# Layer 3 of a four-layer image network: a 3x3 convolution with 12 products in place of 18, and its weights mixed earlier

## The chip, the cores and the metric

The kernel runs on one core of one Trainium2 chip, in float32 throughout. The metric is the device time of one execution in microseconds (us), the median of several runs. The engines are named as in the profile: PE (TensorE, matrix products; PEld is its loading of weights), DVE (VectorE), ACT (ScalarE), POOL (GpSimd) and SP (SyncE, which here issues DMA transfers). Products are accumulated in PSUM banks and moved to SBUF by DVE or ACT, which is called an eviction. A transfer is issued by the queue of an engine; the SP and ACT queues are hardware queues (q1 and q10 of the profile), the POOL queue is a software queue (q0).

## The reference

Eight images of 512 channels and 32x32 positions go through four layers.

- Layer 0: group norm, q, k, v (512x512 each), attention with 8 heads, three steps `hf = hf + 0.1 * tanh(hf @ inl_w.T + inl_b)`, a projection, and the input added.
- Layer 1: attention over the 1024 positions with 64-wide queries and keys, and the input added.
- Layer 2: upsampling by 2 with a 12-tap filter, a leaky ReLU, downsampling by 2.
- Layer 3, a bottleneck block whose weights are different for each image. This is the layer that changes:

```python
pooled = x.mean(axis=(2, 3))
rw = jax.nn.sigmoid(pooled @ router_w.T + router_b)     # 8 numbers per image
W = jnp.einsum('be,eoihw->boihw', rw, experts)          # inside _cond_conv: 8 experts mixed
out = relu(bn1(conv 1x1, 512 -> 128, with W of w1))
out = relu(bn2(conv 3x3, 128 -> 128, with W of w2))
out = bn3(conv 1x1, 128 -> 512, with W of w3)
return relu(out + x)
```

Per image the mixed weights have 512 + 9 x 128 + 512 = 2176 columns on 128 partitions; one expert set is 128 x 2176, all eight are 8.9 MB.

## The kernel before, in words

**Order of the work.** `tile_sequence` handles the images one after the other through layers 0, 1 and 2 (the loop at L1112). Each image's result z is written to device memory in layer 2; image 7's stays in SBUF. Then layer 3 runs for all eight images (L1253 to L1297). A scheduler orders the instructions of each engine by the program's order and by the buffers that are free; only some stretches are fixed by hand. Each engine takes its own instructions strictly in order. The whole program exists a second time (`shifted=True`), which is run only if a range check fails (`out_of_bounds`, L1218); it does not run on these inputs.

**The large products.** q, k, v, the inner steps, the projection and v of layer 1 go through `product` (L404). It computes a 1024x512x512 product from seven block products, in the order P1, C11, U2, U3, C22, C21, C12, in three pairs of PSUM banks: A for P1 and C11, X for U2, U3 and C21, Y for C22 and C12. After each block product `made` evicts two banks. For q and k (`channels`, L453) P1 and C11 go through ACT and the rest through DVE; U2 and U3 are DVE additions of P1's copy (L467). For v (`positions`, L478) all of it goes through DVE; P1 needs two additions of a bias row for each half (L503, L504). An eviction that comes late holds up the next block product in the same bank. Each of q, k, v takes 24 us of PE.

**Weights of `product`** are summed once, for image 0, and stored in device memory over the POOL queue; POOL does parts of the summing itself (L364, L367). Later images load them over the SP queue (`weight`, L340).

**Layer 2's operators** (`layer2_constants`, L133) are matrices that hold the filter taps. They are built from counters (POOL `iota`), the taps, and some 60 small DVE operations (L158 to about L200), called at L847, at the end of image 0's layer-1 scores. `xT` (L857) follows on PE: each bank is emptied by a DVE addition (L858).

**Layer 3.** `route(0, 7)` (L1167) makes the eight mixing numbers of images 0 to 6: a mean, a matmul with the router's weights (L1174), a spreading to all partitions (L1185), a bias (L1189), a sigmoid on ACT (L1193). The scheduler puts it into image 7's layer 1. All experts are loaded once into SBUF by SP (`load_experts`, L1134; the pieces w1, w2_0, w2_1, w2_2 and w3), during image 7's layers 1 and 2, into buffers as these come free. `mixed(b)` (L1204) mixes the weights for one image: per piece one scaling on ACT (L1211) and seven multiply-adds on DVE (L1213), 5 + 35 instructions. It is called one image ahead, and the scheduler begins image 0's during image 7's layer 2, between its DVE evictions (L1003). Per image, PE then does:

- c1: two halves of 4 products each (`project`, L324), relu on ACT into the inside of a zero-rimmed image, of which there are two;
- c2: for each half of the rows 9 products of 128x128 with 128x512, one for each filter tap (L1272), relu on ACT;
- c3: four blocks of two products (L1286); DVE adds the scaled result to z (L1293), ACT applies the relu (L1296), SP writes the output (L1297).

Each f32 matmul appears twice in the records of the profile: 288 records at L1272 are 144 products, 18 for each of 8 images. The buffers that matter: `big`, 7 of 16 KB a partition; `tmp`, 6 of 2 KB or 4 KB; PSUM pools `ps_sc` (two pairs of banks), `ps_tp` and `ps_mm` (two banks each).

Of the kernel before, what the change touches and what calls it, by code (L numbers as in the profile page):

```python
# [9 lines left out]
F32 = mybir.dt.float32  # L10
BF16 = mybir.dt.bfloat16
AF = mybir.ActivationFunctionType
ALU = mybir.AluOpType
# [24 lines left out]
QR = C // 2  # L38
PARTS = ("A11", "A12", "-A22", "S1", "S2", "S3", "S4")
# [14 lines left out]
def tile_sequence(ctx: ExitStack, tc: tile.TileContext, a: dict, out: bass.AP, shifted: bool):  # L54
# [78 lines left out]
    def layer2_constants():  # L133
# [9 lines left out]
        def iota(name, pattern, base, per_partition=0):  # L143
            t = scratch(name, pattern[0][1])
            nc.gpsimd.iota(
                t, pattern, base=base, channel_multiplier=per_partition,
                allow_small_or_imprecise_dtypes=True,
            )
            return t
# [15 lines left out]
        taps_up = scratch("taps_up", NTAP)  # L165
        nc.gpsimd.dma_start(taps_up, a["up_filter"].partition_broadcast(P))
        nc.vector.tensor_scalar_mul(taps_up, taps_up, 2.0)
        taps_dn = scratch("taps_dn", NTAP)
        nc.gpsimd.dma_start(taps_dn, a["down_filter"].partition_broadcast(P))

        part = iota("part", [[1, 1]], 0, 1)
        tap = iota("tap", [[1, NTAP]], 0)

        def rows_of(name, width):

            row = scratch(f"row_{name}", 1)
            first = iota(f"first_{name}", [[width, (P - 1) // width]], width)
            nc.vector.tensor_scalar(first, first, part, None, ALU.is_le)
            nc.vector.tensor_reduce(row, first, AX.X, ALU.add)
            col = scratch(f"col_{name}", 1)  # L180
            nc.vector.scalar_tensor_tensor(col, row, float(-width), part, ALU.mult, ALU.add)
            return row, col

        def tap_index(name, n, step, base, mul, by):

            t = iota(f"ix_{name}", [[step, n]], base)
            add = scratch(f"add_{name}", 1)
            nc.vector.tensor_scalar_mul(add, by, float(mul))
            nc.vector.tensor_scalar_add(t, t, add)
            return t  # L190

        def outer(op, rows, cols):
# [16 lines left out]
        ur = placed("ur", tap_index("ur", UR, -1, 17, -2, in_r), taps_up)  # L209
        outer(up_op, ur, placed("uc", tap_index("uc", UC, 1, 11, -2, in_c), taps_up))  # L210
        outer(
            up_left_op, ur, placed("ucl", tap_index("ucl", UC, 1, 11 - 2 * EDGE, -2, in_c), taps_up)
# [4 lines left out]
            placed("dr", tap_index("dr", OR, 2, -6, 1, up_rr), taps_dn),  # L217
            placed("dc", tap_index("dc", OC, 2, 0, -1, up_cc), taps_dn),
# [4 lines left out]
            placed("ur63", tap_index("ur63", 1, 0, 10, -2, in_r), taps_up),  # L223
            placed("uc63", tap_index("uc63", 2 * W, 1, 5, -2, in_c), taps_up),
# [3 lines left out]
            placed("dr63", iota("dr63", [[2, 3]], 1), taps_dn),  # L228
            placed("dc63", tap_index("dc63", W, 2, 6, -1, part), taps_dn),
# [19 lines left out]
    pooled = const.tile([P, CC, B], F32, name="pooled")  # L249
    spilled = [spill.tile([C, S], F32, name=f"spill_{run}_{b}", tag=f"spill_{b}") for b in range(B)]  # L250
# [338 lines left out]
    def layer0(b, x, norm, w):  # L589
# [12 lines left out]
        if b == 0:  # L602
            nc.vector.tensor_add(row_bias, row_bias, bias2)
        w["inl"] = weight("inl", b)
        all_of(product(f"k_{b}", w["k"], h, t, channels(f"k_{b}", k, qkv_b[:, CC : 2 * CC])))
        w["proj"] = weight("proj", b)
        early = small.tile([P, 1], F32, tag="early", bufs=1, name=f"early_{b}")
        tc.keep_in_program_order(nc.scalar.activation(early, eps, AF.Exp))
        all_of(product(f"v_{b}", w["v"], h, t, positions(f"v_{b}", v, v_row), rows=True))
        w["v1"] = weight("v1", b)  # L610
        hf = big_tile(f"hf_{b}", [P, CC, S])
# [157 lines left out]
    def layer1(b, x, w, midway):  # L769
# [77 lines left out]
        if b == 0:  # L847
            layer2_constants()
# [249 lines left out]
    with tc.tile_pool(name=f"weights_{run}", bufs=1) as wpool:  # L1098
        w = {}
        held = {"q": weight_quarters("q", tmp("raw_q", S))}  # L1100
# [8 lines left out]
        late_loads()  # L1109

# [20 lines left out]
    WCOLS = 2 * C + 9 * P  # L1131
    experts = {}

    def load_experts(key, n, pool=None):  # L1134
        if pool is None:
            t = big_tile(f"{key}e", [P, NE, n])
        else:
            t = pool.tile([P, NE, n], F32, name=f"{key}e", bufs=1)
        nc.sync.dma_start(t, a[key])
        experts[key] = t  # L1140
# [6 lines left out]

    load_experts("w1", C, pool3)

# [11 lines left out]
    router_w = pool3.tile([P, CC, NE], F32, name="router_w", bufs=1)  # L1161
    nc.gpsimd.dma_start(router_w, a["router_wT"].rearrange("(cc p) e -> p cc e", p=P))
    router_b = pool3.tile([P, NE], F32, name="router_b", bufs=1)
    nc.gpsimd.dma_start(router_b, a["router_b"].partition_broadcast(P))
    rw = const.tile([P, B, NE], F32, name="rw")

    def route(b0, b1):  # L1167

        n = b1 - b0
        mean = pool3.tile([P, CC, n], F32, name=f"mean_{b0}", bufs=1)  # L1170
        nc.vector.tensor_scalar_mul(mean, pooled[:, :, b0:b1], 1.0 / S)
        ps = bank(ps_tp, f"router_{b0}")
        for cc in range(CC):
            nc.tensor.matmul(  # L1174
                ps[0:n, 0:NE], mean[:, cc, :], router_w[:, cc, :],
                start=(cc == 0), stop=(cc == CC - 1),
            )

        apart = pool3.tile([n, n, NE], F32, name=f"apart_{b0}", bufs=1)
        nc.vector.tensor_tensor(  # L1180
            apart, ident[0:n, 0:n].unsqueeze(2).to_broadcast([n, n, NE]),
            ps[0:n, 0:NE].unsqueeze(1).to_broadcast([n, n, NE]), ALU.mult,
        )
        ps = bank(ps_tp, f"routed_{b0}")
        nc.tensor.matmul(  # L1185
            ps[:, 0 : n * NE], ones[0:n, :], apart.rearrange("k b e -> k (b e)"),
            start=True, stop=True,
        )
        nc.vector.tensor_tensor(  # L1189
            rw[:, b0:b1, :], ps[:, 0 : n * NE].rearrange("p (b e) -> p b e", e=NE),  # L1190
            router_b.unsqueeze(1).to_broadcast([P, n, NE]), ALU.add,
        )
        nc.scalar.activation(rw[:, b0:b1, :], rw[:, b0:b1, :], AF.Sigmoid)  # L1193

    route(0, B - 1)


    rims = []
    for i in range(2):
        t = pool3.tile([P, H + 2, W + 2], F32, tag=f"rim_{i}", bufs=1, name=f"rim_{i}")  # L1200
        nc.gpsimd.memset(t, 0.0)
        rims.append(t)

    def mixed(b):  # L1204
        wt = pool3.tile([P, WCOLS], F32, tag="mixed", name=f"mixed_{b}")
        parts = [("w1", 0, C)]
        parts += [(f"w2_{ky}", C + ky * 3 * P, 3 * P) for ky in range(3)]
        parts += [("w3", C + 9 * P, C)]
        for key, at, n in parts:
            src, dst = experts[key], wt[:, at : at + n]  # L1210
            nc.scalar.activation(dst, src[:, 0, :], AF.Copy, scale=rw[:, b, 0:1])  # L1211
            for e in range(1, NE):
                nc.vector.scalar_tensor_tensor(  # L1213
                    dst, src[:, e, :], rw[:, b, e : e + 1], dst, ALU.mult, ALU.add
                )
        return wt
# [19 lines left out]
    z3 = {}  # L1236

    def freed(t):
        if t == 4:
            load_experts("w2_0", 3 * P)  # L1240
            z3[0] = load_z(0)
        elif t == 6:
            for ky in (1, 2):
                load_experts(f"w2_{ky}", 3 * P)
        elif t == 7:
            load_experts("w3", C)

    z_last = layer2(B - 1, halo, freed)
    z_next = z3[0]
    redo = None if shifted else out_of_bounds()  # L1250
    wt_next = mixed(0)
    route(B - 1, B)
    for b in range(B):  # L1253
        z, wt = z_next, wt_next
        if b + 1 < B:
            z_next = load_z(b + 1) if b + 2 < B else z_last
            wt_next = mixed(b + 1)
        h1 = rims[b % 2]
        for g in range(2):
            ps = bank(name=f"c1_{b}_{g}")  # L1260
            project(ps, wt[:, 0:C].rearrange("p (cc o) -> p cc o", o=P), 0, z, g)
            nc.scalar.activation(
                h1[:, 1 + 16 * g : 17 + 16 * g, 1 : W + 1],
                ps.rearrange("p (h w) -> p h w", w=W),
                AF.Relu, bias=bn[0][1], scale=bn[0][0],
            )
        h2 = tmp(f"h2_{b}", S)
        banks = [bank(name=f"c2_{b}_{g}") for g in range(2)]
        for ky, g in ((0, 0), (1, 0), (0, 1), (1, 1), (2, 0), (2, 1)):
            for kx in range(3):  # L1270
                at = C + (3 * ky + kx) * P
                nc.tensor.matmul(  # L1272
                    banks[g].rearrange("p (h w) -> p h w", w=W), wt[:, at : at + P],
                    h1[:, ky + 16 * g : ky + 16 * g + 16, kx : kx + W],
                    start=(ky == 0 and kx == 0), stop=(ky == 2 and kx == 2),
                    skip_group_check=True,
                )
        for g in range(2):
# [87 lines left out]
```

## Time and profile before

| | |
|---|---|
| three runs | 3779.12, 3780.01, 3781.69 us; median 3780.01 |
| the profiled execution | 3779.3 us |
| its span, first to last instruction | 3777.5 us, so 1.8 us lie outside |
| mean granted PE clock | 0.997 |
| busy: PE, DVE, ACT, POOL | 3733.1, 2550.6, 1200.6, 85.2 us |
| image 1's q, k, v start | 462.2, 486.2, 510.2 us |
| layer 3: first c1, last c3 ends | 3529.6, 3767.2 us |

How to read the lines: a line such as "L1272 PE MATMUL c<-rim,mixed 128*128 128x512 f32 x288 | 125.5, 593 | 0.0" gives the code line, the engine, the operation, the output and the inputs by the program's names, the tile shapes, the count of instructions, their busy time in us and the mean duration of one in ns, and the idle time of the engine just before them. In the timeline and in the chain of waits the first two figures are the start and the duration in us; "[6.97 <-DVE up L1003]" says that the engine had stood idle 6.97 us until DVE's instruction of L1003 released it. In the table of busy times by stretch, each engine's busy time is followed by its count of instructions, in the order PE, PEld, DVE, ACT, POOL; then come the granted clock, the share of time in which the DMA engines were busy, and GB/s. Rows of single lines give the duration of one instruction as minimum/median/maximum in ns.

### The profile page before, as it was taken

The page shows a single profiled execution, that of the slowest core. Times are in us where ns is not written, and L with a number is a line of the kernel's source. Part 1 is how long each engine was busy: PE and PEld are TensorE (multiplying, and loading weights), DVE is VectorE, ACT ScalarE, POOL GpSimd, SP SyncE. Part 2 cuts the span into 40 slices and gives each one's busy share as a digit, 9 for nine tenths or more (in the row PEclk, how much of TensorE's full clock was granted, in tenths as well). Part 3 has the DMA queues.
Part 4 walks back from the last instruction along what each step waited for, and adds up shares of the span by engine and source line. Part 5 has one row for each costly group of instructions (what it writes and reads, how often), then busy time and mean ns, then how long its engine had stood idle before and what let it go on. Part 6 is the DMA issues. An engine that isn't in the chain of part 4 may idle for free.

```text
span 3777.5 us, 50171 instructions
## 1 busy us (share of the span) xinstructions
PE 3733.1 (99%) x20838; PEld 1985.0 (53%) x20838; DVE 2550.6 (68%) x3589; ACT 1200.6 (32%) x1716; POOL 85.2 (2%) x115
## 2 busy tenths in 40 slices
PE   8999999999999999999999999999999999998998
PEld 4346653475435753476534754367534754357543
DVE  4877548665676648765586657766487656866885
ACT  1631225212442216312352125422262133421332
POOL 4000000000000000000000000000000000001000
PEclk9999999999999999999999999999999999999999
DMA  5002310122101320013101220023201131004432
GB/s 205 21 3 85 120 59 1 52 79 96 40 1 64 120 81 1 17 70 120 59 1 62 96 88 21 1 81 105 80 1 42 65 119 40 1 1 132 157 152 94
DMA packets 86193, 248.67 MB, mean 66 GB/s; under 512 B 10480, under 2 KB 33024, under 8 KB 79168
## 3 DMA queue, kind: packets, MB, share of 16 engines
q1 hardware_dynamic: 70528, 221.67, 16.6%
q10 hardware_dynamic: 13824, 12.59, 1.0%
q0 software_dynamic: 1600, 11.07, 0.8%
q8 instruction: 166, 2.72, 0.3%
q14 instruction: 75, 0.61, 0.1%
HBM read 185.40 MB, written 59.90 MB: 65 GB/s over the span
## 4 chain that ended last, share of the span: by engine, by line
PE 96%; DVE 2%; DMA 1%; issue 0%; ACT 0%; POOL 0%; SPq 0%; ACTq 0%; DVEq 0%; POOLq 0%
PE scores L640 12%; PE av L681 12%; PE inl_X L435 7%; PE up L1019 5%; PE dn L1037 5%; PE inl_A L435 4%; PE v_X L435 4%; PE inl_Y L435 4%; PE av_X L953 4%; PE c L1272 3%; PE v_A L435 3%; PE v_Y L435 3%; PE av_Y L953 3%; PE av_A L953 3%; PE proj_X L435 2%; PE q_X L435 2%
## 5 line engine op out<-in xcount | busy, mean ns | idle before, releaser
L659 ACT ACTIVATE e<-scores 128x1024 f32<-128x1024 f32 x504 | 516.2, 1024 | 668.3 <-PE scores L640 661.4
L640 PE MATMUL scores<-q,k 64*64 64x512 f32 x4096 | 532.1, 592 | 0.0
L681 PE MATMUL av<-e,v 64*64 64x512 f32 x4096 | 528.8, 589 | 0.0
L665 DVE TENSOR_TENSOR acc<-acc,e 128x1024 f32<-128x1024 f32 x320 | 389.3, 1216 | 37.4 <-ACT e L659 35.4
L640 PEld LDWEIGHTS scores<-q,k 64*64 64x64 f32 x4096 | 150.7, 133 | 295.2 <-issue 216.8
L681 PEld LDWEIGHTS av<-e,v 64*64 64x64 f32 x4096 | 156.8, 133 | 282.7 <-issue 276.7
L435 PE MATMUL inl_X<-T_hf,w_inl 128*128 128x512 f32 x576 | 261.6, 592 | 0.0
L1003 DVE SCALAR_TENSOR_TENSOR up<-up,leak 128x512 f32<-128x512 f32 x264 | 173.8, 687 | 125.9 <-ACT leak L1002 120.9
L702 DVE RECIPROCAL inv<-av 128x256 f32<-128x256 f32 x128 | 223.0, 1747 | 2.0 <-PE av L694 2.0
L1002 ACT ACTIVATE leak<-up 128x512 f32<-128x512 f32 x264 | 149.8, 596 | 206.1 <-DVE up L1003 132.9
L1037 PEld LDWEIGHTS dn<-dn_op,up 128*64 128x64 f32 (+1 forms) x4096 | 187.9, 136 | 18.2 <-issue 18.2
L1037 PE MATMUL dn<-dn_op,up 128*64 128x99 f32 (+5 forms) x4096 | 194.0, 253 | 0.0
L1019 PE MATMUL up<-halo,up_op 126*128 126x512 f32 (+1 forms) x384 | 182.0, 601 | 9.4 <-DVE up L1003 9.4
L435 PEld LDWEIGHTS inl_X<-T_hf,w_inl 128*128 128x128 f32 x576 | 108.8, 190 | 138.4 <-issue 112.2
L435 PE MATMUL inl_A<-hf,w_inl 128*128 128x512 f32 x384 | 174.3, 597 | 0.0
L531 ACT ACTIVATE inl_U<-inl_U,inl_b 128x512 f32<-128x512 f32 x96 | 66.7, 718 | 302.7 <-DVE inl_U L546 302.7
L663 DVE TENSOR_TENSOR acc<-e,e 128x1024 f32<-128x1024 f32 x64 | 79.4, 1240 | 107.2 <-ACT e L659 92.4
L542 DVE TENSOR_TENSOR inl_U<-inl_X,inl_P 128x512 f32<-128x512 f32 x96 | 61.8, 685 | 113.9 <-PE inl_X L435 112.9
L1272 PE MATMUL c<-rim,mixed 128*128 128x512 f32 x288 | 125.5, 593 | 0.0
L1019 PEld LDWEIGHTS up<-halo,up_op 126*128 126x128 f32 (+1 forms) x384 | 72.0, 191 | 97.3 <-issue 66.3
L435 PEld LDWEIGHTS inl_A<-hf,w_inl 128*128 128x128 f32 x384 | 71.6, 190 | 97.2 <-issue 86.5
L953 PE MATMUL av_A<-v,eT 128*128 128x256 f32 x512 | 122.3, 384 | 0.0
(299 smaller groups left out, 5534.5 us busy)
## 6 DMA issues: line engine op xcount, KB each, us to landing
halo<-ypad_u SPq DMA_DIRECT2D x128, 252.0 KB
halo<-ypad_u SPq DMA_DIRECT2D x128, 198.0 KB
w_v<-stored_u_v SPq DMA_DIRECT2D x14, 1792.0 KB
x<-in_x_dram SPq DMA_DIRECT2D x32, 512.0 KB
spill_u<-z SPq DMA_DIRECT2D x28, 512.0 KB
z<-spill_u SPq DMA_DIRECT2D x28, 512.0 KB
out_dram<-z SPq DMA_DIRECT2D x28, 512.0 KB
w_q<-stored_u_q SPq DMA_DIRECT2D x7, 1792.0 KB
```

What stands on the lines that cost most here:

```text
L435: nc.tensor.matmul(dst, lhs, rhs, start=(opens and s == 0 and cc == 0), stop=(cc == 1 and s == rows), skip_group_check=True,)
L640: nc.tensor.matmul(ps[r][rows[c]], k[rows[r], oc, jc * P + c * HD : jc * P + c * HD + HD], q[rows[r], oc, ts(sh, HALF)], start=True, stop= ...
L659: nc.scalar.activation(e, pair, AF.Exp, scale=HD ** -0.5)
L665: nc.vector.tensor_add(accs[g], accs[g], e)
L681: nc.tensor.matmul(avs[g][r][rows[c]], v[rows[r], jc, ts(2 * oc + c, HD)], e[rows[r], ts(c, HALF)], start=(jc == 0), stop=(jc == SC - 1),)
L702: nc.vector.reciprocal(copies[g][:, at], totals[g][:, at])
L953: nc.tensor.matmul(ps[:, ts(s, QR)], left[:, j, at : at + P], right[:, j, :], start=(what in ("P1", "U2", "W") and s == 0 and j == 0), sto ...
L1002: nc.scalar.mul(t, ps, 0.2 * SQRT2)
L1003: nc.vector.scalar_tensor_tensor(dst, ps, SQRT2, t, ALU.mult, ALU.max)
L1019: nc.tensor.matmul(ps[i], op[0 : IR * n, :], halo.tile(t)[0 : IR * n, c + i, :], start=True, stop=True,)
L1037: nc.tensor.matmul(rows[part, r0 - first : r1 + 1 - first, c0 : c1 + 1], up[t][0:k, c, ts(2 * cc + s, HD)], op[:, r0 - 4 * t + 3 : r1 + 4 ...
L1272: nc.tensor.matmul(banks[g].rearrange("p (h w) -> p h w", w=W), wt[:, at : at + P], h1[:, ky + 16 * g : ky + 16 * g + 16, kx : kx + W], st ...
```

## The change

**12 products for 18.** Two neighbouring outputs of a row are computed from four products of sums. With d0..d3 the four inputs that two outputs of a row need and g0, g1, g2 a filter row, the sums of the data are d1 + d2, d3 - d1, d2 - d1, d0 - d2 (`spread`, four DVE operations over the whole rimmed image, reading every second column), and the filter's are (g0 + g2) / 2 +- g1 / 2, g0 and g2 (`load_weights`: one ACT, three DVE operations for each image). Each kind is summed over the three filter rows: 4 x 3 products for both halves. Two copies (`one`, `two`) and two DVE operations make the odd outputs; the even ones need none. c3's results are then in the order even/odd, and its evictions write with a step of two.

**The mixing moves.** `route(b-1)` stands after q of image b, `premix(b-1)` is divided over image b's k and v: nine chunks, each loaded from device memory by the POOL queue into one of two halves of a large buffer, scaled on ACT, and added up by seven DVE operations. The result goes to device memory over the POOL queue, and `load_weights` fetches it in layer 3 over SP. Every image reads all 8.9 MB of experts again. Image 7's mixing lies in layer 3, two chunks after c3 of each of the first five images.

**Moves besides.** The router's weights are loaded at the start. Layer 2's operators are called between image 0's q and k, with their counters and taps at the very start. The range check moves to the second image of layer 3. PE's order in layer 3 is written by hand: c2's three parts, c1 of the next image's first half, c2's last part, c1's second half, c3.

```diff
+    def premix(b):
+        read = big_tile(f"experts_{b}", [P, 2, NE, QR])
+        for first in range(0, WX, S):
+            total = min(S, WX - first)
+            acc = tmp(f"mix_{b}_{first}", S)
+            for at in range(0, total, QR):
+                n = min(QR, total - at)
+                src = read[:, (at // QR) % 2, :, 0:n]
+                nc.gpsimd.dma_start(src, a["experts"][:, :, first + at : first + at + n])
+                dst = acc[:, at : at + n]
+                nc.scalar.activation(dst, src[:, 0, :], AF.Copy, scale=rw[:, b, 0:1])
+                for e in range(1, NE):
+                    nc.vector.scalar_tensor_tensor(
+                        dst, src[:, e, :], rw[:, b, e : e + 1], dst, ALU.mult, ALU.add
+                    )
+                yield
+            nc.gpsimd.dma_start(mixed[b][:, first : first + total], acc[:, 0:total])
...
         if b == 0:
             nc.vector.tensor_add(row_bias, row_bias, bias2)
+            with suppress(StopIteration):
+                operators.send(t[3][1][:, 0:1])
+        else:
+            route(b - 1)
+            mixing = premix(b - 1)
+            for _ in range(3):
+                next(mixing)
         w["inl"] = weight("inl", b)
         all_of(product(f"k_{b}", w["k"], h, t, channels(f"k_{b}", k, qkv_b[:, CC : 2 * CC])))
         w["proj"] = weight("proj", b)
+        if b:
+            for _ in range(3):
+                next(mixing)
...
         all_of(product(f"v_{b}", w["v"], h, t, positions(f"v_{b}", v, v_row), rows=True))
         w["v1"] = weight("v1", b)
+        if b:
+            all_of(mixing)
...
-        if b == 0:
-            layer2_constants()
...
+    def load_weights(b):
+        wt = pool3.tile([P, WU], F32, tag="weights", name=f"weights_{b}")
+        u = wt[:, C : C + 12 * P].rearrange("p (y s o) -> p y s o", y=3, s=4)
...
+            nc.sync.dma_start(dst, src)
+        g0, g1, g2, even = (u[:, :, i, :] for i in range(4))
+        nc.scalar.mul(g1, g1, 0.5)
+        nc.vector.tensor_add(even, g0, g2)
+        nc.vector.scalar_tensor_tensor(even, even, 0.5, g1, ALU.mult, ALU.subtract)
+        nc.vector.scalar_tensor_tensor(g1, g1, 2.0, even, ALU.mult, ALU.add)
...
+    def spread(b):
+        d = [rim[:, :, k : k + W - 1 : 2] for k in range(4)]
+        t = pool3.tile([P, 4, (H + 2) * W // 2], F32, tag="spread", bufs=1, name=f"spread_{b}")
...
+        nc.vector.tensor_add(to[1], d[1], d[2])
+        nc.vector.tensor_sub(to[3], d[3], d[1])
+        nc.vector.tensor_sub(to[2], d[2], d[1])
+        nc.vector.tensor_sub(to[0], d[0], d[2])
...
+            c2(b, main, 1, True, False)
+            nc.scalar.copy(one, main)
+            c2(b, odd, 3, True, True)
+            c2(b, main, 2, False, False)
+            nc.scalar.copy(two, main)
+            nc.vector.scalar_tensor_tensor(one, one, 2.0, two, ALU.mult, ALU.subtract)
+            nc.vector.tensor_add(one, odd, one)
...
+            if more:
+                c1(b + 1, 0)
+            c2(b, main, 0, False, True)
...
+            if more:
+                c1(b + 1, 1)
+                spreads[b + 1] = spread(b + 1)
+            if b == 0:
+                route(B - 1)
+                mixing = premix(B - 1)
+            elif b == 1 and not shifted:
+                redo = out_of_bounds()
+            c3(b, h2)
+            if b < 5:
+                for _ in range(2):
+                    next(mixing, None)
```

## The prediction

> **What bounds the kernel now.** First the page's busy shares: TensorE is at work for 99% of the span, so a removed matmul is worth its full time as long as nothing else then becomes late. The group of the 3x3 convolution gives the count, 288 records.
>
> ```profile
> PE 3733.1 (99%) x20838; PEld 1985.0 (53%) x20838; DVE 2550.6 (68%) x3589; ACT 1200.6 (32%) x1716; POOL 85.2 (2%) x115
> L1272 PE MATMUL c<-rim,mixed 128*128 128x512 f32 x288 | 125.5, 593 | 0.0
> ```
>
> Then the chain that ended last, around layer 3's second image. It is an unbroken row of matmuls; an image repeats after 3597.20 - 3567.73 = 29.47 us. An f32 matmul leaves two records, so 36 records are 18 products, and one product is 15.45 / 18 = 0.858 us of the chain.
>
> ```profile
> 3561.73 6.01 PE c L324 x14
> 3567.73 15.45 PE c L1272 x36
> 3583.19 0.86 PE c L1286 x2
> ...
> 3597.20 15.45 PE c L1272 x36
> ```
>
> Then busy times by stretch: image 1's q, k, v, and one image of layer 3.
>
> ```profile
> 462.16:486.19 24.03, 24.03 (x57) 10.31 (x57) 9.96 (x14) 3.20 (x6) 0.00 (x0) 1.00 0.22 87
> 486.19:510.22 24.03, 24.03 (x57) 10.55 (x56) 6.80 (x10) 4.03 (x6) 0.00 (x0) 1.00 0.21 77
> 510.22:534.30 24.08, 24.08 (x113) 21.09 (x111) 10.52 (x16) 0.00 (x0) 0.00 (x0) 1.00 0.21 76
> 3559.05:3588.50 29.45, 29.44 (x70) 12.78 (x69) 26.15 (x39) 10.21 (x14) 0.00 (x0) 1.00 0.37 143
> ```
>
> The third figure with a count after the length is VectorE: 26.15 of 29.45 us in layer 3. Were the 6 products merely dropped, an image would last 24.3 us of TensorE against 26 of VectorE: the mixing has to leave. In k and v VectorE has 17.2 + 13.6 us free. TensorE is idle nowhere there, so every late eviction shows in the total.
>
> Last, who TensorE waits for: two of the longest waits lie in code that moves.
>
> ```profile
> PE up L1019 <- DVE up L1003: 9.4, 9, 7.0
> ...
> PE xT L857 <- DVE y L858: 5.2, 1, 5.2
> ```
>
> **The change part by part**, against the profiled execution (3779.3 us: span 3777.5 and 1.8 around it; 0.7 under the median of the runs).
>
> *Twelve products for 18.* 8 images x 6 x 0.858 = **-41.2 us**, if layer 3 stays on TensorE. VectorE per image: 4 `spread` operations and 2 on the sums at 0.7 (an addition of 128x512 takes 0.69; the `spread` reads skip columns and could take double), 3 on weights at 0.61, 4 evictions at 1.28: 11.2 us, and 14 premix operations in the first five images, 6.2: 17.4 of 24.3. Double-priced spreads add 3 and still fit. ScalarE: 10.2 us now, less 2.5 of mixing, plus 2 copies at 0.58, 0.6 and 2 scales at 0.5: 10.5. Inside an image, `two`, sum, addition and relu (0.58 + 0.75 + 0.69 + 0.78 = 2.8) lie beside c1(b+1,0) and main0, 3.4 + 2.6; the spread (0.78 + 0.75 to its first use) beside c3(b), 6.9. That cover is gone twice: at the start c1(0,1), relu, spread, first c2 follow each other, 1.53 plus hand-overs, **+1.75**; in the last image 2.8 us stand against main0's 2.6 plus the copy, **+0.85**.
>
> *Image 7's layer 1 and 2.* The mixing of image 0 ran ahead of the upsampling's evictions on VectorE:
>
> ```profile
> 3470.82 5.63 DVE L1213 SCALAR_TENSOR_TENSOR mixed<-w1e,rw,mixed 128x512 f32<-128x512 f32 x8
> ...
> 3476.37 0.68 DVE L1003 SCALAR_TENSOR_TENSOR up<-up,leak 128x512 f32<-128x512 f32 x1
> ...
> 3478.46 2.08 PE L1019 MATMUL up<-halo,up_op 126*128 126x512 f32 x2 [6.97 <-DVE up L1003]
> ```
>
> It is gone: **-7.0**; with the 7-image routing (0.35 + 0.35) **-0.7**. What would be late next is the halo transfer, 1.5 us in this stretch, already counted in the row's neighbours.
>
> *Layer 3's loads.* z and output are 4 MB an image, weights 1.1, mixing 2 MB more in five images: 7.1 MB in 24.3 us is 292 GB/s. Now an image runs at 143 GB/s with the DMA engines busy 0.37, so by that share 292 GB/s is 0.75: it fits, but the premix scale on ScalarE and its operations on VectorE sit in order before evictions, and wait for their chunk. Below: 0. Above: 1 us for each of 8 images, a hand-over's size. I take **+2**.
>
> *Image 0.* layer2_constants (some 60 small VectorE operations, 17 us) held up L858 for 5.2 us; that goes. They now stand between q's evictions, while GpSimd sums weights, 17.8 us busy between 20 and 44. In one place of the trace the two meet:
>
> ```profile
> 338.28 1.30 POOL L837 TENSOR_TENSOR seen<-seen,acc 128x512 f32<-128x512 f32 x1 [51.67 <-DVE acc L829]
> 338.29 1.33 DVE L189 TENSOR_SCALAR setup<-setup 128x32 f32<-128x32 f32 x1
> ```
>
> A scaling of 32 columns lasted 1.33 us, exactly beside GpSimd's 1.30. About 20 of them precede q's U3 evictions; if a third meet a sum, 8 us. Bounds: -5 (all hidden) to +8. I take **+4** net.
>
> *Routing of image b-1 after q, 7 times.* TensorE: 0.28 + 0.32 for a single image (L1174, L1185 near 3542). ScalarE's sigmoid (0.21) and two scales stand before k's copy of P1 (0.58, L463), for which C11's bank waits: 0.36. **7 x 0.95 = +6.7**; bounds 0 (it replaces no idle time, so a gain is excluded) and 10.
>
> *Premix, 7 times.* An image's mixing is 8 chunks of 256 columns and one of 128, 7 VectorE operations each. Of the form, the trace has 512 and 384 columns:
>
> ```profile
> L1213 DVE SCALAR_TENSOR_TENSOR mixed<-w1e,rw,mixed x56: 741/745/752, 3464.7 to 3716.8; 128x512 f32<-128x512 f32 x56
> L1213 DVE SCALAR_TENSOR_TENSOR mixed<-w_0e,rw,mixed x56: 601/609/619, 3506.8 to 3717.4; 128x384 f32<-128x384 f32 x56
> ```
>
> Their difference is 0.136 for 128 columns, so 256 takes 0.47, and 0.42 follow on follow: 2.95 a chunk, 24.5 an image, and 31 us are free in k and v. It fits on average. What can be late is the load: 1 MB by GpSimd's queue, in rows of 1 KB, two buffers, so chunk n+2 starts when chunk n is done. Nearest rows (last figure: us from issue to landing):
>
> ```profile
> stored_u_v<-w_v POOLq DMA_DIRECT2D x2, 1792.0 KB, 7.7
> stored_u_q<-w_q POOLq DMA_DIRECT2D x1, 1792.0 KB, 6.0
> ...
> router_w<-in_router_wT_dram POOLq DMA_DIRECT2D x1, 16.0 KB, 2.2
> ```
>
> 16 KB lands in 2.2; 1 MB adds some 2.9 at the 46 ns of a 1 KB packet in the trace on 16 engines: L = 5.1, bounds 2.2 and 7.7. Two chunks per L + 0.5 + 2.95: 4.3 us a chunk, 9 chunks 38 us of 48. But VectorE and ScalarE take their work in order: the operations of chunk 5 stand before v's P1 evictions (two additions of 0.69 within 1.72 us), of 6 to 8 before U3, C12 and the attention's first exponential. When a chunk comes late, all of that is, and TensorE without a free bank. Below: 0. Above: a whole chunk and both ends of a late load, 6 us. I take 2, nearer to 0 since the chain has 10 us to spare: **7 x 2 = +14**.
>
> One rule speaks against this. The Trainium skill, page "SBUF — State Buffer", section "SBUF: two separate sides", says that the descriptors of a transfer issued from GpSimd's queue are written by GpSimd through a port pair that it shares with VectorE, that a VectorE operation in a two-port mode locks it out for its whole length, and that a transfer of 620 ns was seen to take 3100 ns so; it advises a hardware queue. The meeting at 338.3 agrees with the lock; no row shows a load delayed by it. Were each load 2.5 us later by that figure, L would be 7.6, nine chunks 50 us, and the estimate of the sum 3774.
>
> **Sum**: -41.2 + 1.75 + 0.85 - 7.0 - 0.7 + 2 + 4 + 6.7 + 14 = -19.6: **3760 us**.
>
> **The rivals.**
> (a) *All the mixing is hidden.* 31 us free on VectorE and 10 to spare in the load chain speak for it; the in-order queues against. Premix 0, routing 0.6 x 7 = 4.2, image 0 at -4: 3779.3 - 46.3 + 2 - 4 + 4.2 = 3735.
> (b) *Slower: the reload chain.* Without its term the sum is 3746; 0.2% (7.6 us, about what a measurement of this kernel tells from no change) over 3779.3 is reached at 41 / 7 = 5.9 us per image. Nine chunks must then take 48 + 5.9 us, 6 a chunk, so L is 8.5 us, above the slowest row of 7.7, which moves 1.8 times as much; at L = 9, 8 us an image, 3802. The place: chunks 5 to 9 in v, VectorE waiting in front of its evictions.
> (c) *Layer 3 does not follow TensorE any more.* Weights, z, output and two chunks collide, and ScalarE's queue stands on a load: at 2 us an image, 3760 + 14 = 3774, at 3 us no gain. For it: 292 GB/s is twice today's rate. Against: the DMA engines are busy 0.37.
>
> **Numbers.** Forecast (3745 to 3771) 0.50; (a) 0.25; (b) 0.11; (c), with image 0 or the premix at mid-bounds, 0.14. The likeliest case gives 3760. The range, 8 in 10, reaches down to (a) with its constants cheaper, 3731, and up through (c) to premix at 5.5 us an image, 3785. Faster by over 0.2% (under 3771.7): 0.50 + 0.25 and a little of (c), 0.77; within: 0.12; slower: 0.11.
>
> **What would show it.** Layer 3 in steps of 24.3 us in the chain, with the first c2 some 1.7 us after c1; no 7 us wait at the upsampling of image 7; TensorE waiting for VectorE in q of image 0, by a few us in all; in v of images 1 to 7 waits of some 2 us for the additions L503, with VectorE standing on loads of experts. Wrong would be: loads that land in over 8 us, k and v over 52 us together (then b), none of these waits (then a), or c1 and c2 of layer 3 waiting for ScalarE (then c).

## The result and the profile after

The changed kernel takes 3825.68 us (median of 4 runs, 3822.75 to 3826.40) against 3780.57 us before (median of 4): a ratio of 1.0118, 95% interval 1.0101 to 1.0136. It is 45 us slower where the forecast said 20 us faster. The profiled execution's span is 3824.5 us, 47.0 more than before. The page of the changed kernel, busy shares and the chain that ended last:

```profile
PE 3726.7 (97%) x20802; PEld 1983.0 (52%) x20802; DVE 2644.5 (69%) x3905; ACT 1237.3 (32%) x1785; POOL 162.9 (4%) x210
...
PE 86%; DMA 6%; DVE 6%; issue 1%; ACT 1%; POOL 0%; SPq 0%; POOLq 0%; ACTq 0%; DVEq 0%
PE av L743 11%; PE scores L702 11%; PE inl_X L485 6%; DMA experts<-in_experts_dram 5%; PE up L1079 5%; PE dn L1097 5%; PE inl_A L485 4%; PE av_X L1013 4%; PE inl_Y L485 4%; PE av_Y L1013 3%; DVE mix L295 3%; PE av_A L1013 3%; PE v_X L485 3%; PE proj_X L485 2%; PE q_X L485 2%; PE v_Y L485 2%
```

A load of experts is now on the chain, and PE's share of it fell from 96% to 86%. PE has 48 products less, 41 us of work, yet its busy time fell by 6.4 us only: 60 records of routing came in, and some of the remaining work ran slower, at half the clock (below). Who PE waits for, in the changed kernel (us in total, times, longest):

```profile
PE v_X L485 <- DVE v_U L561: 32.9, 14, 4.8
PE gn_mean L345 <- DVE mv L339: 10.7, 1, 10.7
PE c L1286 <- DVE z L1295: 8.0, 6, 2.2
PE scores L702 <- DVE v L568: 8.0, 7, 1.4
PE c L1286 <- DVE mix L295: 7.2, 1, 7.2
PE q_X L485 <- DVE q_U L517: 6.2, 1, 6.2
PE v_A L485 <- DVE v_P_hi L554: 4.2, 7, 1.1
```

All but the second are new. Where the 47 us lie, by the starts of q, projection and c1 in the two traces: up to image 1's q +0.2 (before, its first product starts at 461.9 us, 0.3 ahead of the figure in the table); six images of 446.9 us in the mean in place of 436.3, +63.9; image 7 to the first c1 +2.8; layer 3 to the end of the span 228.0 in place of 247.9, -19.9.

Inside an image all of the loss lies between the start of q and the projection, in image 1 267.9 us in place of 257.4. Busy times by stretch for image 1's q, k, v and for one image of layer 3, as shown of before:

```profile
462.11:486.75 24.64, 24.64 (x67) 10.62 (x65) 10.54 (x16) 4.49 (x7) 0.00 (x0) 1.00 0.42 152
486.75:512.17 25.42, 25.35 (x64) 11.17 (x61) 17.83 (x40) 4.56 (x9) 2.64 (x3) 1.00 0.51 169
512.17:543.80 31.63, 26.45 (x111) 21.52 (x109) 22.55 (x45) 3.52 (x6) 4.32 (x6) 0.95 0.64 214
3720.72:3746.38 25.66, 24.30 (x57) 10.56 (x56) 12.76 (x20) 9.62 (x13) 0.56 (x1) 1.00 0.36 129
```

v takes 31.6 us for 24.1, 5.2 of them with PE idle, and DVE is busy for 22.6 of 31.6: not full. The clock's mean there is 0.95. Layer 3's image has shrunk from 29.5 to 25.7 us, not to 24.3, and its chain, unbroken matmuls before, now runs through DVE:

```profile
3734.62 3.45 PE c L374 x8
3738.15 0.79 ACT rim L1255
3739.60 0.72 DVE spread L1266
3741.59 1.21 DVE z L1295
3742.84 3.70 PE c L1286 x8
3746.54 7.72 PE c L1275 x18
```

Now image 2's v, where the idle time comes from: first the transfers issued around chunk 6 and ACT's scaling of it, then DVE:

```profile
958.98 0.32 SPq L394 DMA_DIRECT2D w_proj<-stored_u_proj  x1
...
959.54 0.57 POOL L299 DMA_DIRECT2D mixed_u<-mix  x1 [3.04 <-DVE mix L295]
960.10 0.92 POOL L291 DMA_DIRECT2D experts<-in_experts_dram  x1
...
970.75 0.51 ACT L293 ACTIVATE mix<-experts,rw 128x256 f32<-128x256 f32 x1 [8.44 <-DMA experts<-in_experts_dram]
```

```profile
971.29 1.28 DVE L295 SCALAR_TENSOR_TENSOR mix<-experts,rw,mix 128x256 f32<-128x256 f32 x3 [3.97 <-ACT mix L293]
...
974.99 0.68 DVE L561 TENSOR_TENSOR v_U<-v_X,v_P 128x512 f32<-128x512 f32 x1
```

and PE in the same stretch:

```profile
975.73 5.41 PE L485 MATMUL v_X<-w_v,T_h 128*128 128x256 f32 x16 [3.51 <-DVE v_U L561]
...
983.27 3.72 PE L485 MATMUL v_X<-w_v,T_h 128*128 128x256 f32 x16 [0.84 <-DVE v_U L561]
```

Read from the top: chunk 6 was issued at 960.10, just behind the 1.8 MB of w_proj and the 0.5 MB store of mixed columns, and its scaling could begin 10.6 us later; DVE stood idle for 3.97 us at a multiply-add of that chunk, with v's eviction (L561) queued behind it; PE, whose bank that eviction empties, waited 3.51 us. PE's two lines are the second loss: the same 16 records took 5.41 us after that wait and 3.72 later. The busy times by stretch of the changed kernel say why, in the column of the granted clock (the figure after POOL's count): it was halved for one stretch of 3.4 us.

```profile
973.20:976.60 3.40, 0.88 (x4) 0.80 (x5) 3.31 (x7) 0.00 (x0) 0.40 (x1) 1.00 0.66 188
976.70:980.00 3.30, 3.30 (x9) 2.66 (x8) 0.52 (x2) 0.51 (x1) 0.88 (x1) 0.50 0.66 187
980.10:983.50 3.40, 2.56 (x12) 1.95 (x11) 3.29 (x7) 0.26 (x1) 0.00 (x0) 1.00 0.64 231
```

### The profile page after: what moved, and what is told of

It is laid out like the page before. It is cut to its first block, busy times and chain, and to the rows that moved or that the text cites. A ratio compares the mean times of both kernels' runs of the same rounds, so it can differ in the third digit from the quotient of the medians.

```text
span 3824.5 us, 50832 instructions
## 1 busy us (share of the span) xinstructions
PE 3726.7 (97%) x20802; PEld 1983.0 (52%) x20802; DVE 2644.5 (69%) x3905; ACT 1237.3 (32%) x1785; POOL 162.9 (4%) x210
## 4 chain that ended last, share of the span: by engine, by line
PE 86%; DMA 6%; DVE 6%; issue 1%; ACT 1%; POOL 0%; SPq 0%; POOLq 0%; ACTq 0%; DVEq 0%
PE av L743 11%; PE scores L702 11%; PE inl_X L485 6%; DMA experts<-in_experts_dram 5%; PE up L1079 5%; PE dn L1097 5%; PE inl_A L485 4%; PE av_X L1013 4%; PE inl_Y L485 4%; PE av_Y L1013 3%; DVE mix L295 3%; PE av_A L1013 3%; PE v_X L485 3%; PE proj_X L485 2%; PE q_X L485 2%; PE v_Y L485 2%
## 5 line engine op out<-in xcount | busy, mean ns | idle before, releaser
L727 DVE TENSOR_TENSOR acc<-acc,e 128x1024 f32<-128x1024 f32 x320 | 389.1, 1216 | 36.6 <-ACT e L721 34.6
L295 DVE SCALAR_TENSOR_TENSOR mix<-experts,rw,mix 128x256 f32<-128x256 f32 (+1 forms) x504 | 219.8, 465 | 114.6 <-ACT mix L293 108.8
L293 ACT ACTIVATE mix<-experts,rw 128x256 f32<-128x256 f32 (+1 forms) x72 | 34.8, 494 | 320.7 <-DMA experts<-in_experts_dram 320.4
L485 PE MATMUL v_X<-w_v,T_h 128*128 128x256 f32 x384 | 102.1, 422 | 32.9 <-DVE v_U L561 32.9
```

The source lines that it names most:

```text
L295: nc.vector.scalar_tensor_tensor(dst, src[:, e, :], rw[:, b, e : e + 1], dst, ALU.mult, ALU.add)
L485: nc.tensor.matmul(dst, lhs, rhs, start=(opens and s == 0 and cc == 0), stop=(cc == 1 and s == rows), skip_group_check=True,)
L727: nc.vector.tensor_add(accs[g], accs[g], e)
```

## The experiments

The theories: **A**, loads of chunks land late, and the instructions that wait for them stand on the in-order queues of ACT and DVE ahead of evictions; **B**, the mixing's work is too much for DVE in k and v; **C**, GpSimd's software queue is what is slow. "An image" below is the time from one q to the next; on the chips of these runs the kernel before took 3781 to 3782 us.

**No mixing in q, k, v.** Removed: the calls of `route` and `premix` in `layer0`; `load_weights` reads expert 0 for images 0 to 6.

> The changed kernel without routing and premix of images 0 to 6; layer 3 takes expert 0 as their weights (the mixing of those images is left out), image 7's stays. In the changed kernel an image repeats after 446.6 us, before after 436.4. Theories A (late chunk loads stand ahead of evictions) and B (VectorE's added work itself delays evictions) both expect 436.4 us an image, no half-clock stretches in v, layer 3 as in the changed kernel, and 3826 - 7 x 10.2 = 3754 us in all (3750 to 3758). If images stay above 438, something other than mixing was added to q, k, v.

3748.1 us in one run, an image 436.3 in the mean, as before the change: what was added to q, k, v is all of their loss. This doesn't tell A from B. Layer 3 stayed bad, with a wait of 7.1 us for image 7's mixing.

**The work, without the reloads.**

```diff
-                nc.gpsimd.dma_start(src, a["experts"][:, :, first + at : first + at + n])
+                if first + at < 2 * QR:
+                    nc.gpsimd.dma_start(src, a["experts"][:, :, first + at : first + at + n])
```

> The changed kernel with all its scalings, multiply-adds and stores of premix, but only the first two chunks of an image are loaded; the other seven read these two again (so the mixed weights are wrong from column 512 on). In layer 3 too. Theory A, late loads: the waits of TensorE for v_U (33 us in all) go, an image takes 436.4 plus 0.6 of routing plus 0.5 to 2 of interleaved work, and the time falls by 7 x 8.5 and some 10 in layer 3, to 3745 to 3770. Theory B, VectorE's work: images stay at 444 to 447, time 3810 to 3826.

3742.0 us in one run. Image 2 from q to projection, busy times of this run:

```profile
898.50:1156.82 258.32, 258.32 (x1446) 111.39 (x1443) 196.10 (x270) 101.89 (x136) 1.68 (x3) 1.00 0.11 41
```

PE is busy in all 258.32 us, although DVE does all 63 multiply-adds (196.1 us of work, before 171.7). B falls. The routing and all of the hidden mixing cost 258.32 - 257.34 = 0.98 us an image.

**The loads on SyncE's queue** (`nc.sync.dma_start` in `premix`).

> The changed kernel with the chunk loads issued by SyncE's hardware queue in place of GpSimd's. Theory C, the software queue is what makes a chunk late (0.9 us of GpSimd for each, descriptors held up by VectorE): from issue to ScalarE's scaling 6.1 us becomes some 4.5, and the time falls by 3 to 5 us an image, to 3790 to 3805. Theory A, the chain of two buffers and the transfers beside it: 5.5 to 6 us, still 10 where a weight load of 1.8 MB goes ahead, time 3812 to 3835; slower is possible where a chunk that waits for its buffer holds up later loads of SyncE.

3783.6 us, ratio to before 1.0004 (0.9994 to 1.0014), so some 42 us faster than the change; better than either theory expected. From issue to scaling chunks 3, 5, 7 and 8 took 5.6 to 6.1 us (medians over images) against 6.1 to 6.2 on GpSimd's queue: C is worth some 0.3 us a chunk. The 2.5 us a load that the prediction worked out from the Trainium skill's page "SBUF — State Buffer", section "SBUF: two separate sides", did not come in these loads. But chunk 6 took 7.3 instead of 10.8 (medians again): on SyncE's queue the 1.8 MB of w_proj are issued 0.6 us behind that chunk, not 1.1 us ahead of it. How much of the 42 us each of the two is worth, this run doesn't tell. PE's waits for DVE became short:

```profile
PE v_X L485 <- DVE v_U L561: 19.6, 14, 1.8
```

and with none over 1.8 us in v, no stretch of half clock came in any of the images 1 to 7; in the changed kernel each has one.

**The operators back in layer 1** (the `operators.send` moved from after q to after `all_of(values)`).

> The changed kernel with the layer-2 operators' VectorE work back at the end of image 0's layer-1 scores (counters and taps still at the start). q of image 0 takes 25.7 us in place of 35.3; the wait at xT and the half clock after it come back, 9.6 us between image 0's projection and image 1's q. If both are the same mechanism moved, the total is 3824 to 3828; if the stall in q has also pushed something else, it falls below 3820.

3820.7 us, ratio 1.0102 (1.0085 to 1.0119), between the two expectations and, by its interval, not to be told from the change. q to projection of image 0 fell from 268.6 to 258.7 us, and the wait at xT came back, 4.2 us, with 7.0 us more from the projection to image 1's q: most of the same loss, in another place.

**w_proj loaded after v** (a DVE copy of one column of v's last block into the tile holds the load back).

> The changed kernel, chunk loads on GpSimd's queue as in it, but the load of w_proj (1.8 MB) waits for v's last block product instead of starting at v's first; it is used 180 us later. Theory A in the form 'chunk 6 shares the DMA engines with w_proj and the store of the mixed columns' (10.7 us from issue to scaling, others 6.1): chunk 6 takes 6 to 7.5 us, the wait of 3.5 us at v_X goes with its half clock, 4 to 6 us an image, time 3785 to 3800, near the run with SyncE's queue (3784), whose gain then came from the same order. Theory C, the software queue by itself: chunk 6 stays above 9 us and the time above 3812.

3824.0 us: no gain, the expectation failed. Chunk 6 did take 6.8 us, and the waits for v_U halved (17.2 us). But w_proj and w_v1 now load together at the end of v, and the store of the mixed columns lands late beside them; the attention's exponentials need its buffer. Waits of PE and one line of ACT's timeline in this run:

```profile
PE scores L707 <- ACT e L726: 17.8, 7, 3.0
PE v_X L487 <- DVE v_U L563: 17.2, 8, 2.6
```

```profile
1000.96 1.94 ACT L726 ACTIVATE e<-scores 128x1024 f32<-128x1024 f32 x2 [4.84 <-DMA mixed_u<-mix]
```

**Four chunks ahead.**

```diff
-        read = big_tile(f"experts_{b}", [P, 2, NE, QR])
+        reads = [big_tile(f"experts_{b}_{i}", [P, 2, NE, QR]) for i in range(2)]
...
-                src = read[:, (at // QR) % 2, :, 0:n]
+                i = (first + at) // QR
+                src = reads[i // 2 % 2][:, i % 2, :, 0:n]
```

> The changed kernel with two large buffers for the experts, so four chunks ahead in place of two; queue and order as in it. Theory A, a chain of two buffers whose loads are waited for in order: nearly all waits in v go, an image takes 437 to 439 us, time 3755 to 3772. Theory C, the software queue or the rate of the DMA engines: 9 MB in 80 us is no problem for the engines, but a queue that needs 6 us a chunk would still be late from chunk 6 on: time 3785 to 3810.

3745.8 us, ratio 0.9906 (0.9886 to 0.9926): 36 us faster than before, some 80 faster than the change, by one more buffer. Image 2 from q to projection has no idle time left:

```profile
899.00:1157.30 258.30, 258.30 (x1446) 111.47 (x1443) 196.05 (x269) 102.29 (x136) 7.89 (x10) 1.00 0.19 67
```

The queue is still GpSimd's and from issue to scaling chunks 5 to 9 take even longer (6.0 to 9.8 us, medians), but they are no longer waited for. The time is below the range given to A; image 7's chunks in layer 3 are early now too (that wait of 7.2 us is gone, and from the first c1 to the end it is 217.0 us in place of 228.0).

**The spread behind two evictions** (in `c3`, after the second block, in place of ahead of c3).

> The changed kernel with the four spread operations of the next image after the second of c3's evictions in place of ahead of the first; nothing else. If these 2.5 us on VectorE ahead of the eviction are why c3's third block waits 1.36 us an image, layer 3's images without mixing repeat after 24.3 us in place of 25.66, and the time falls by 7 to 10, to 3816 to 3819. If the evictions with a step of two are too slow themselves, the steps stay above 25 us.

3819.0 us in one run. An image of layer 3 without mixing took 24.5 us (3739.57 to 3764.07) in place of 25.66 (3720.72 to 3746.38), and the 8.0 us of waits for z became 1.1. As expected.

**Mixing begun in q** (`route` and three chunks after q's second block product, three before k, the rest before v).

> The changed kernel, two buffers and GpSimd's queue as in it, with routing and the first three chunks after q's second block product instead of after q, three more before k and the rest before v: the chain of nine chunks, 59 us in the changed kernel, begins some 15 us earlier. Two forms of theory A are told apart. Length: the chain was longer than the 48 us of k and v, and what was left over met v and the attention; then 15 us more clear most of it, time 3755 to 3785. Order: each late chunk stands ahead of whichever eviction follows it on VectorE, so the waits move from v into q and k; then 3800 to 3826.

3861.4 us, ratio 1.0205 (1.0175 to 1.0235): slower still, and slower than either form expected. Nine chunks began 18 us earlier and ended 14 us earlier, and the waits only moved:

```profile
PE k_A L485 <- ACT k_P L513: 35.7, 7, 5.7
PE v_A L485 <- DVE v_P_hi L554: 34.0, 7, 5.1
```

The first line is ACT's: a chunk's scaling, waiting for its load, stands ahead of the copy of k's P1. So an earlier start does not clear the waits: they went to the evictions that now stand behind the late chunks, as the form "order" has it.

**The filter alone, mixing left in layer 3** (`mixed` and `load_experts` of before with the new c1, c2, c3).

> The changed kernel's 12 products in layer 3 with the mixing where it was before: routing of images 0 to 6 together and experts loaded once into SBUF, mixed one image ahead in layer 3; nothing is mixed in q, k, v. (The mixed columns for c1 and c3 lie in another buffer to fit.) By the rows of before VectorE needs 7 x (2 x 0.667 + 3 x 0.53) = 20.5 us of mixing and 11.2 of the new layer 3 an image, 31.7 against TensorE's 24.3: an image takes 31 to 32.5 us instead of 29.5, and the time is 3790 to 3810. If VectorE overlaps better than its rows say, up to 41 us are gained: 3740 to 3775.

3788.6 us, ratio 1.0016 (1.0004 to 1.0027), just under the first expectation. An image of layer 3 takes 30.4 us (the mean of five), against 29.5 before, with DVE at work nearly throughout (the third busy time):

```profile
3590.00:3620.00 30.00, 25.31 (x59) 10.09 (x58) 29.87 (x50) 11.33 (x15) 0.00 (x0) 1.00 0.36 140
```

So the filter gains nothing while the mixing is beside it.

**Two buffers, order by hand.** `premix` yields after each multiply-add; ACT and DVE are scheduled by hand in k and v:

```diff
+            made = product(f"k_{b}", ...)
+            for n in (14, 0, 4, 0, 4, 4, 1):
+                next(made)
+                some(n)
...
+            for n in (0, 7, 1, 0, 4, 5, 5):
+                next(made)
+                some(n)
...
+                if 3 <= i < 20:
+                    some(1)
```

`some(n)` emits n multiply-adds behind a block product's evictions; the last lines are in the attention's loop.

> The changed kernel, two buffers and GpSimd's queue as in it, but VectorE's and ScalarE's order in k and v of images 1 to 7 written by hand: each chunk's multiply-adds stand behind the evictions that come before its load has landed (6.1 us after its buffer is free), and chunks 8 and 9 go one multiply-add per step into the attention. Same loads, same work, same memory. Theory A in the form order (a chunk's wait stands ahead of evictions): the waits in v go although every load is as late as before, an image takes 437 to 440 us, time 3750 to 3775. If the depth of the buffers itself was what helped in the run with four, images stay above 443 and the time above 3795.

3801.2 us, ratio 1.0052 (1.0029 to 1.0074), and an image 443.6 us: by these two numbers it is the second expectation, the depth, that came. But nearly all of the waits in v went, as the first has it, and a new one stood in the attention: waits of PE, then lines of PE and ACT:

```profile
PE scores L714 <- ACT e L733: 18.7, 7, 2.8
...
PE v_X L488 <- DVE v_U L564: 6.6, 7, 0.9
```

```profile
994.40 1.45 PE L714 MATMUL scores<-q,k 64*64 64x512 f32 x8 [2.76 <-ACT e L733]
```

```profile
992.93 0.51 ACT L293 ACTIVATE mix<-experts,rw 128x256 f32<-128x256 f32 x1 [4.49 <-DMA experts<-in_experts_dram]
```

Chunk 8 was issued at 982.75, w_v1 at 982.93, and its scaling was written too early. One number was changed, `3 <= i < 20` to `9 <= i < 26`:

> As the run with the hand-written order, with one number changed: chunks 8 and 9 enter the attention from its tenth step instead of its fourth. In that run the waits in v had gone (45 us in all to 6.6), and a new one of 2.8 us an image stood at the attention's fourth step: chunk 8's load, 10.2 us beside the 1.8 MB of w_v1, held up ScalarE's exponentials. If that is all that was left, an image falls from 443.6 to 438 to 440 us, with no half-clock stretch, and the time to 3752 to 3775. If two buffers cost time in themselves, images stay above 442.

3770.0 us, ratio 0.9970 (0.9955 to 0.9984), an image 439.2 us, as the expectation of order alone had it. Image 2 from q to projection, with PE idle for 1.2 us and no halved clock:

```profile
903.30:1163.60 260.30, 259.14 (x1446) 111.13 (x1443) 197.74 (x269) 102.09 (x136) 7.92 (x10) 1.00 0.19 67
```

Same loads, same two buffers, same work as in the changed kernel: some 56 us less by order alone, the multiply-adds of the last two chunks being put off into the attention.

**What the runs point to, together.**

> The changed kernel with what the runs so far point to: four chunks deep, chunk loads on SyncE's queue, w_proj loaded after v, spread after c3's second eviction, and layer 2's operators after image 0's first block products of k, when GpSimd's sums are nearly over. By theory A all of the wait in v, of c3 and of image 0 goes: 3742 of the run without reloads, less 8 (layer 3), less 9 (image 0), plus a few us of layer 3's own loads: 3722 to 3738, 1.1 to 1.6% under the kernel before.

3733.5 us, ratio 0.9875 (0.9859 to 0.9892), 48.6 us under before on the same chip and the fastest kernel here. Beyond the start of the program, the longest of PE's waits in it, summed by line, are:

```profile
PE up L1085 <- DVE up L1069: 2.4, 8, 0.9
PE q_A L488 <- DVE h L367: 2.0, 1, 2.0
```

## Why the prediction was wrong

| step of the prediction | predicted us | measured us |
|---|---|---|
| 12 products, layer 3's start, end and loads | -36.6 | -19.9 |
| image 7's layers 1 and 2 | -7.7 | -8.3 |
| image 0 | +4 | +0.2 |
| routing | +6.7 | +6.9 |
| premix | +14 | +69.4 |
| rest | | -1.3 |
| sum | -19.6 | +47.0 |

(Image 7's figure is its 2.8 us less the 11.1 that its own q to projection lost. Routing is 7 x 0.98 from the run without reloads, the hidden mixing included. Premix is what images 1 to 7 lost from q to projection, 76.3, less that.)

**The step that failed is "Premix, 7 times"**: "I take 2, nearer to 0 since the chain has 10 us to spare". An image lost 9.9 us, beyond the upper bound of 6, and the outcome, slower, had been given a chance of 0.11. The place was right: chunks 5 to 9 in v, DVE waiting in front of its evictions. Wrong was the price, in two ways.

First, spare time of the chain was taken as a cover for waits, but it covered none here: each engine takes its work in order. Nine chunks took 59 us, not 38, since a chunk's load took 6.1 us, not 5.1, and 10.8 where w_proj and the store shared the DMA engines, and since its multiply-adds are mixed with evictions that wait for PE in turn. Yet this length was not it either: begun 18 us earlier, the chain cost more. Rival (b) put the turning point at a load of 8.5 us in every chunk; with most loads at 6.1 and the order as scheduled the kernel was already past it. Its sign of k and v over 52 us together came (57.1 us in image 1), that of loads over 8 us in chunks 4 and 6 alone (8.2 and 10.8, medians). What decides is whether a waiting instruction stands ahead of an eviction: with two buffers and another order an image takes 439.2 us, with four 437.0, with the scheduler's order and two 446.9.

Second, a wait of PE was counted at its length. Of the 69.4 us, 45.1 are waits (32.9 + 8.0 + 4.2). In images 1 to 7 the clock was halved for 27.3 us, which costs up to 13.7 more. The remaining 10.7 or so were not traced to a cause; gaps too short to be listed as waits, under 0.15 us, make up 0.6 of them.

**Layer 3** fell short by 16.7 us. The step of 24.3 us an image is what PE is busy for (24.30 of 25.66 us in the row above), and the whole term of -36.6 is near what can be had: the combined version's layer 3, from the first c1 to the end of the last c3, is 202.1 us against 237.6, a gain of 35.5 with start and loads in it. DVE's sum of 11.2 us was near too (12.8 measured, 2.7 of it the last chunk of image 7's mixing), but an average again: the next image's spread, 2.5 us, stood ahead of c3's first eviction, 1.36 us an image. And rival (c), ACT's queue standing on a load, came once, in the second image, for 7.2 us with a halved clock around it; that image took 35.7 us, and 25.6 in the run without reloads. The lines, PE and ACT of the changed kernel:

```profile
3656.94 10.09 PE L1286 MATMUL c<-h,weights 128*128 128x512 f32 x16 [7.22 <-DVE mix L295]
```

```profile
3647.30 0.51 ACT L293 ACTIVATE mix<-experts,rw 128x256 f32<-128x256 f32 x1 [6.66 <-DMA experts<-in_experts_dram]
```

**Image 0**: the meeting of DVE and GpSimd was the right mechanism. Three small scalings took 7.17 us beside GpSimd's sums, two others took 0.40 after them (DVE, then PE of the changed kernel):

```profile
30.90 7.17 DVE L201 TENSOR_SCALAR setup<-setup 128x16 f32<-128x16 f32 x3
...
39.35 0.40 DVE L201 TENSOR_SCALAR setup<-setup 128x64 f32<-128x64 f32 x2
```

```profile
41.40 5.38 PE L485 MATMUL q_X<-T_h,w_q 128*128 128x512 f32 x8 [6.15 <-DVE q_U L517]
```

From q to projection image 0 lost 9.8 us so, the wait of 6.15 and a half clock. But the wait at xT that went was worth 9.6, not 5.2: it too had a half clock at it (from 349.1 to 355.9 us before). So the two cancel, where +4 was to be left. **Routing**, with the hidden mixing in its figure, and **image 7's upsampling** were right to within 1 us.

## What to carry to other kernels

Work hidden in the gaps of an in-order engine is hidden only if nothing it waits for is late: ask for each waiting instruction what stands behind it, not whether the sums fit. Spare time on average, or an earlier start, didn't help here; a deeper buffer or an order with the waiting work behind the evictions did. Where PE bounds a kernel, price a wait of some microseconds with the half clock that comes with it.

## What the runs showed of the hardware

- The clock was halved in stretches of 3.41, 6.83 or 10.24 us, and waits well under 3.41 us can bring one. Over the runs here every wait of PE from 2.7 us up came with one, except the one of 10.5 to 11.9 us at the start of the program; of those from 1.8 to 2.7 us some did (2.20 us in the changed kernel's layer 3 did, 8 records then taking 5.40 us in place of 3.70; 2.17 in the run four chunks deep did not), and of shorter ones none, but for one stretch with the filter alone, behind a row of small routing products and waits of up to 1.17 us. The Trainium skill's page "TensorE: Matmul & The Clock Gate", section "HAM oscillation — how this bites in real kernels", says to avoid idle gaps over about 3.4 us; these runs put the bound lower, for the most part between 1.8 and 2.7.
- Large transfers share the DMA engines whatever their queues: from issue to use, 1 MB on GpSimd's queue took 6.1 us alone, 10.8 beside 1.8 MB on SyncE's and 0.5 MB on its own, and 6.8 with the 1.8 MB held back. Holding them back moved the collision to the next transfers, for no gain.
